# Two MoE blocks on one core: the chosen experts' rows are added to the shared expert's part by accumulating transfers instead of by GpSimd

## The chip, the cores and the metric

The kernel runs on one core of one Trainium2 chip. The time is the device time of one execution in microseconds; the median over a few executions is given, and one further execution was recorded by the hardware profiler. Engine names are those of the profile: PE is the matrix engine, PEld its weight loads, DVE the vector engine, ACT the scalar engine, POOL is GpSimd, SP the queue that issues most transfers. An entry such as SPq or POOLq is the queue of that engine.

## What is computed

The input is 32 sequences of 256 tokens with 128 features, so 8192 tokens. Two layers follow one another. Each normalises x, forms an attention part s and a mixture-of-experts part g, and adds their product to x. Cut to what matters here:

```
xn = layernorm(x)
s  = linear_attention(xn)              # layer 0: 16 heads, causal product of two scores
shared   = 0.1 * (gelu(xn @ sw_up + sb_up) @ sw_down + sb_down)
combined = sum over the 2 chosen of 8 experts of 0.1 * weight * expert(xn)
out = shared + combined
g   = silu(out / (max|out| + 1e-6))
x   = x + s * g
xn = layernorm(x)
s  = sparse_softmax_attention(xn)      # layer 1
g  = silu(mixture_with_capacity(xn))   # layer 1, top 2 of 8 experts
x  = x + s * g
```

The change touches the line `out = shared + combined` of layer 0 and the order of the work around it.

## The kernel before, in words

The tokens are cut into NP = 16 blocks of PT = 512 tokens; a block is a tile of 128 partitions with TT = 4 rows of 128 features, 128x512 numbers or 256 KB. Layer 0 goes like this.

**Attention of layer 0** (`attention0`) is one generator that is advanced in 256 small steps, 16 for each block. A step holds some transposes and products on PE, copies on ACT (`qk`, line 777) and multiplications on DVE (`feat`, line 744; `pat`, line 792). The whole kernel is written as such generators, and the code advances them in turn. Attention writes s and the shared expert's part of each block to DRAM as `part[p]`.

**Routing and dispatch** send each token's row to both chosen experts by indirect transfers from the POOL queue.

**The experts** (`experts`) take 71 tiles of 256 rows, and scatter the weighted results with indirect transfers (line 166) to `moe0` in DRAM, which has one row for each token and choice: first choice in rows 0 to 8191, second choice after them. Every reader of `moe0` has to wait for all these scatters (`back0.behind`).

**The combination of layer 0** (`combine0(p)`, one generator for each block) is where the change lies. It runs beside the last 40 steps of attention0, and for its last blocks beside the first steps of layer 1's attention. Its stages before the change are:

- stage 0: SP loads `x` (line 571), `so` with s and the shared part (line 965, 512 KB), and by `read` both rows of `moe0` into the tile `rows` (line 244, two transfers of 256 KB);
- stage 1: POOL adds the two to the shared part, `acc`, in the upper half of `so` (line 971, two instructions);
- stage 2: DVE forms the maximum and its reciprocal, `mx` (lines 974 to 977);
- stage 3: ACT scales `acc` (line 981) and takes the tanh (line 983) into the first half of `rows`; POOL multiplies s by `acc` (line 984);
- stage 4: DVE forms s times g (line 986), POOL adds x (line 987) and stores the new x to `x1` in DRAM (line 988);
- stages 5 to 7: the layernorm of layer 1: statistics on DVE (993 to 997), a power on POOL (998), the shift on DVE (`lnnb`, 1001), the scaling on ACT (1004);
- stages 8 and 9: transposes on PE (1009), and the routing logits of layer 1 (1019, 1021).

When each stage is written into the instruction streams is given by a plan: stage n of block p comes EVERY*p + LATER[n] steps after the experts' end.

```
EVERY, LATER = 3, (0, 3, 5, 6, 9, 10, 11, 13, 14, 16)
plan = sorted((t0 + EVERY * p + d, p, n) for p in range(NP) for n, d in enumerate(LATER))
```

PE, ACT and DVE keep this order: `inline` ties each instruction to the one written before it on its engine, so an instruction that waits holds up all behind it, those of attention0 too. POOL's instructions and SP's transfers are not tied in this way. A scheduler places them when the kernel is built, by when it believes their data to be there. On the chip each queue then runs strictly in that order.

The tiles `so` and `rows` come from a pool with four buffers. The `so` of block p+4 can be loaded only when line 987 of block p is done with the old one, and `rows` when line 986 is.

After the last block's logits, `route1` does the routing of layer 1; its dispatch and its experts follow, beside attention.

Of the kernel before, what the change touches and what calls it, by code (L numbers as in the profile page):

```python
# [11 lines left out]
F32 = mybir.dt.float32  # L12
# [3 lines left out]
ALU = mybir.AluOpType  # L16
# [4 lines left out]
P = 128  # L21
# [7 lines left out]
PT = 512  # L29
TT = PT // P  # L30
# [27 lines left out]
def model_kernel(ctx: ExitStack, tc: tile.TileContext, a: dict, out: bass.AP):  # L58
    nc = tc.nc
    B = a["x"].shape[0]  # L60
    T = B * S
# [18 lines left out]
    moe0 = dram.tile([2 * T, P], F32, name="moe0")  # L80
# [3 lines left out]
    moe = dram.tile([2 * T, P], F32, name="moe")  # L84
# [155 lines left out]
    def read(back, rows, moe, p):  # L240

        for k in range(2):
            t0 = k * T + p * PT
            get = nc.sync.dma_start(rows[:, k], moe[t0 : t0 + PT, :].rearrange("(n p) c -> p n c", p=P))
            back.behind(get)


    recent = {}
# [7 lines left out]
    def inline(made):  # L256


        if made.ins.engine in recent:
            tc.add_manual_dep(made.ins, recent[made.ins.engine].name, ORDER, reason="in the order given")  # L260
        return note(made)
# [22 lines left out]
    def mm_tile(name):  # L284
        return ps_m.tile([P, 512], F32, tag="mm", name=name)
# [256 lines left out]
    with ExitStack() as c0:  # L542
# [26 lines left out]
        def load(p):  # L569
            x = wk.tile([P, TT, P], F32, tag="x", name="x", bufs=6)  # L570
            nc.sync.dma_start(x, xin[:, p * TT : (p + 1) * TT, :])
            return x
# [123 lines left out]
        back0 = Scatter("results0", moe0)  # L696
# [263 lines left out]
        def combine0(p):  # L960

            t = slice(p * TT, (p + 1) * TT)
            x = load(p)
            so = bk.tile([P, 2, TT, P], F32, tag="soin", name="soin")
            nc.sync.dma_start(so, part[p])
            rows = bk.tile([P, 2, TT, P], F32, tag="rows", name="rows")
            read(back0, rows, moe0, p)
            yield
            acc = so[:, 1]
            for k in range(2):  # L970
                nc.gpsimd.tensor_tensor(acc, acc, rows[:, k], ALU.add)
            yield
            mx = wk.tile([P, TT], F32, tag="mx", name="mx", bufs=4)
            inline(nc.vector.tensor_reduce(mx, acc, AX.X, ALU.max, apply_absolute_value=True))
            inline(nc.vector.tensor_scalar(mx, mx, 1e-6, None, ALU.add))
            inline(nc.vector.reciprocal(mx, mx))
            inline(nc.vector.tensor_scalar(mx, mx, 0.5, None, ALU.mult))
            yield

            for i in range(TT):  # L980
                inline(nc.scalar.activation(acc[:, i, :], acc[:, i, :], AF.Copy, scale=mx[:, i : i + 1]))
            th = rows[:, 0]
            inline(nc.scalar.activation(th, acc, AF.Tanh))
            nc.gpsimd.tensor_tensor(so[:, 0], so[:, 0], acc, ALU.mult)
            yield
            inline(nc.vector.scalar_tensor_tensor(acc, th, 1.0, so[:, 0], ALU.add, ALU.mult))
            nc.gpsimd.tensor_tensor(x, x, acc, ALU.add)
            nc.gpsimd.dma_start(x1[p], x)
            yield
            st = wk.tile([P, TT, 6], F32, tag="lnst1", name="lnst1")  # L990
            mv = wk.tile([P, TT, 2], F32, tag="lnmv1", name="lnmv1", bufs=4)
            for i in range(TT):
                inline(nc.vector.bn_stats(st[:, i, :], x[:, i, :]))
            for i in range(TT):
                inline(nc.vector.bn_aggr(mv[:, i, :], st[:, i, :]))
            rs = wk.tile([P, TT], F32, tag="lnrs1", name="lnrs1", bufs=4)
            inline(nc.vector.tensor_scalar(rs, mv[:, :, 1], EPS, None, ALU.add))
            nc.gpsimd.tensor_tensor(rs, rs, minus[:, :TT], ALU.pow)
            yield
            nb = wk.tile([P, TT], F32, tag="lnnb1", name="lnnb1", bufs=4)  # L1000
            inline(nc.vector.scalar_tensor_tensor(nb, mv[:, :, 0], -1.0, rs, ALU.mult, ALU.mult))
            yield
            for i in range(TT):
                inline(nc.scalar.activation(xn[:, p * TT + i, :], x[:, i, :], AF.Identity,
                                            bias=nb[:, i : i + 1], scale=rs[:, i : i + 1]))
            yield
            pst1 = mm_tile("pst1")
            for i in range(TT):
                inline(nc.tensor.transpose(pst1[:, i * P : (i + 1) * P], xn[:, p * TT + i, :], ident))
            if p < KEEP:  # L1010
                xnT1 = xTs1[:, 2 * p : 2 * p + 2, EDGE : EDGE + S]
            else:
                xnT1 = wk.tile([P, PT], F32, tag="xnT1", name="xnT1").rearrange("p (b s) -> p b s", b=2)
            inline(nc.scalar.copy(xnT1, pst1.rearrange("p (b s) -> p b s", b=2)))
            yield
            psl = mm_tile("psl")
            pl = psl[:, : TT * E].rearrange("p (i e) -> p i e", e=E)
            for i in range(TT):
                inline(nc.tensor.matmul(pl[:, i, :], lhsT=xnT1[:, i // 2, i % 2 * P : (i % 2 + 1) * P], rhs=wg1,
                                        start=True, stop=True))  # L1020
            inline(nc.vector.tensor_copy(logit[:, t, :], pl))
            yield
# [66 lines left out]
        bk = c0.enter_context(tc.tile_pool(name="bk0", bufs=4))  # L1089


        EVERY, LATER = 3, (0, 3, 5, 6, 9, 10, 11, 13, 14, 16)
        t0 = at
        plan = sorted((t0 + EVERY * p + d, p, n) for p in range(NP) for n, d in enumerate(LATER))
        going = {}
# [3 lines left out]
        def results(now):  # L1099
            while plan and plan[0][0] < now and plan[0][1] <= (now - 4) // SPP - 1:  # L1100
                _, p, n = plan.pop(0)
                if n == 0:
                    going[p] = combine0(p)
                next(going[p])
# [64 lines left out]
    with ExitStack() as cm:  # L1169
# [38 lines left out]
        rows = [(e, e * CAP + q * MT) for e in range(E) for q in range(CAP // MT)]  # L1208
# [13 lines left out]
    with ExitStack() as cb:  # L1222
        bk = cb.enter_context(tc.tile_pool(name="bk", bufs=3))

        def combine(p):

            rows = bk.tile([P, 2, TT, P], F32, tag="rows", name="rows")
            read(back1, rows, moe, p)
            x = bk.tile([P, TT, P], F32, tag="xc", name="xc")
            nc.sync.dma_start(x, x1[p])  # L1230
            yield
            y = bk.tile([P, TT, P], F32, tag="yc", name="yc")
            helper = nc.gpsimd if p < NP - 1 else nc.vector
            helper.tensor_tensor(y, rows[:, 0], rows[:, 1], ALU.add)
            th = rows[:, 0]
            nc.scalar.activation(th, y, AF.Tanh)
            nc.scalar.activation(th, th, AF.Identity, bias=1.0)
            yield
            s = att.dst[p]
            helper.tensor_tensor(y, th, y, ALU.mult)  # L1240
            helper.tensor_tensor(y, y, s, ALU.mult)
            helper.tensor_tensor(y, y, x, ALU.add)
            nc.sync.dma_start(outv[:, p * TT : (p + 1) * TT, :], y)
            yield
# [115 lines left out]
```

## The time and the profile before

| | us |
|---|---|
| median of 3 runs | 1929.27 |
| lowest and highest | 1926.44 and 1931.02 |
| the profiled execution, its own time | 1932.48 |
| its span in the profile | 1930.6 |
| busy PE in that span | 1805.7 (94%) |
| busy DVE | 1175.4 (61%) |
| busy ACT | 962.0 (50%) |
| busy POOL | 847.5 (44%) |

The span is the time from the first to the last recorded instruction; 1.9 us of the execution's own time lie outside it. The combination of layer 0 stands between 940 and 1189 us of the span. A share of busy time is a mean over stages with different limits, so this stage has to be read by itself.

### The profile page before, as it was taken

The page shows a single profiled execution, that of the slowest core. Times are in us where ns is not written, and L with a number is a line of the kernel's source. Part 1 is how long each engine was busy: PE and PEld are TensorE (multiplying, and loading weights), DVE is VectorE, ACT ScalarE, POOL GpSimd, SP SyncE. Part 2 cuts the span into 40 slices and gives each one's busy share as a digit, 9 for nine tenths or more (in the row PEclk, how much of TensorE's full clock was granted, in tenths as well). Part 3 has the DMA queues.
Part 4 walks back from the last instruction along what each step waited for, and adds up shares of the span by engine and source line. Part 5 has one row for each costly group of instructions (what it writes and reads, how often), then busy time and mean ns, then how long its engine had stood idle before and what let it go on. Part 6 is the DMA issues. An engine that isn't in the chain of part 4 may idle for free.

```text
span 1930.6 us, 45909 instructions
## 1 busy us (share of the span) xinstructions
PE 1805.7 (94%) x18616; PEld 1394.5 (72%) x18616; DVE 1175.4 (61%) x2227; ACT 962.0 (50%) x2180; POOL 847.5 (44%) x991
## 2 busy tenths in 40 slices
PE   5999999998999999999887799999999799999997
PEld 4777777776888888887765676677777577777765
DVE  6659667665333433443577597888888433335786
ACT  5433333334444544545354575577677333335776
POOL 3001555543444544444545540044544355555454
PEclk8999999999999999999988777999999899999998
DMA  8911211112344443434334410211111122222343
GB/s 279 385 52 31 69 56 43 45 44 67 126 137 125 138 142 125 134 125 137 116 105 143 137 50 7 71 67 34 32 34 33 51 73 67 72 69 84 90 113 101
DMA packets 127524, 183.86 MB, mean 95 GB/s; under 512 B 16340, under 2 KB 83183, under 8 KB 127312
## 3 DMA queue, kind: packets, MB, share of 16 engines
q1 hardware_dynamic: 96096, 92.45, 16.2%
q0 software_dynamic: 28336, 79.73, 12.3%
q10 hardware_dynamic: 2880, 8.74, 1.2%
q8 instruction: 147, 2.41, 0.5%
q14 instruction: 65, 0.53, 0.1%
HBM read 104.11 MB, written 78.00 MB: 94 GB/s over the span
## 4 chain that ended last, share of the span: by engine, by line
PE 31%; ACT 8%; DVE 5%; DMA 2%; issue 2%; POOL 2%; SPq 1%; ACTq 0%; DVEq 0%; POOLq 0%
PE mpsu L1186 6%; PE mpsd L1200 6%; PE apsc L378 3%; PE apsT L406 3%; PE apav L415 3%; ACT apT L408 3%; ACT apr L398 2%; PE apsk L338 2%; PE apsc L384 2%; DMA rows<-moe 1%; PE apsq L350 1%; PE apsv L358 1%; PE mpst L1179 1%; DVE apr L396 1%; DMA soin<-part 1%
## 5 line engine op out<-in xcount | busy, mean ns | idle before, releaser
L166 POOL DMA_INDIRECT moe<-od,to x270 | 270.0, 1000 | 124.3 <-issue 70.8
L777 ACT COPY qk<-ptr 128x512 f32<-128x512 f32 x256 | 138.2, 588 | 241.9 <-PE ptr L775 241.4
L792 DVE TENSOR_TENSOR pat<-pp,dmask 128x1024 f32<-128x1024 f32 x128 | 156.2, 1221 | 109.6 <-PE pp L790 109.6
L395 DVE TENSOR_REDUCE amx<-apsc 128x4 f32<-128x496 f32 x256 | 170.2, 665 | 38.6 <-PE apsc L384 38.5
L408 ACT COPY apT<-apsT 124x512 f32<-124x512 f32 x256 | 142.8, 584 | 100.8 <-PE apsT L406 99.9
L790 PE MATMUL pp<-qk 64*128 64x128 f32 x2048 | 172.6, 297 | 15.8 <-DVE pat L792 14.1
L790 PEld LDWEIGHTS pp<-qk 64*128 64x128 f32 x2048 | 136.8, 194 | 58.4 <-issue 42.5
L396 DVE TENSOR_TENSOR apr<-apsc,amx 128x496 f32<-128x496 f32 x256 | 172.4, 673 | 9.1
L940 ACT ACTIVATE ha<-eup,wt 128x256 f32<-128x256 f32 x284 | 119.0, 471 | 111.8 <-PE eup L935 57.7
L935 PE MATMUL eup<-xdT,wt 128*128 128x256 f32 x568 | 150.2, 390 | 10.8 <-ACT od L954 7.1
L166 POOL DMA_INDIRECT disp<-xr,slot x128 | 132.4, 1034 | 62.7 <-issue 26.7
L744 DVE TENSOR_TENSOR feat<-rot 128x1024 f32<-128x1024 f32 x128 | 157.5, 1272 | 3.9
L406 PE MATMUL apsT<-ident,apr 128*124 128x128 f32 x1024 | 150.7, 293 | 8.3 <-ACT apr L398 3.5
L775 PE MATMUL ptr<-ident,feat 128*128 128x128 f32 x1024 | 146.9, 288 | 7.6 <-DVE feat L744 7.6
L166 POOL DMA_INDIRECT disp<-xr,sidx x128 | 126.7, 990 | 55.0 <-issue 24.7
L415 PE MATMUL apav<-ava,apT 124*64 124x9 f32 x4096 | 143.4, 205 | 0.0
L415 PEld LDWEIGHTS apav<-ava,apT 124*64 124x64 f32 x4096 | 136.8, 140 | 8.8 <-issue 8.4
L948 PEld LDWEIGHTS edn<-wt,ha 128*128 128x128 f32 x1136 | 137.8, 192 | 3.6
L948 PE MATMUL edn<-wt,ha 128*128 128x128 f32 x1136 | 138.1, 275 | 0.0
L775 PEld LDWEIGHTS ptr<-ident,feat 128*128 128x128 f32 x1024 | 114.7, 145 | 29.9 <-issue 13.9
L406 PEld LDWEIGHTS apsT<-ident,apr 128*124 128x124 f32 x1024 | 120.9, 148 | 16.2 <-ACT apr L398 8.8
L935 PEld LDWEIGHTS eup<-xdT,wt 128*128 128x128 f32 x568 | 99.5, 190 | 45.0 <-issue 27.4
(250 smaller groups left out, 3342.8 us busy)
## 6 DMA issues: line engine op xcount, KB each, us to landing
disp<-zero SPq DMA_DIRECT2D x17, 1040.0 KB, 8.5
rows<-moe SPq DMA_DIRECT2D x64, 256.0 KB, 3.9
xd<-disp SPq DMA_DIRECT2D x71, 130.0 KB, 2.3
xd<-disp SPq DMA_DIRECT2D x32, 260.0 KB, 2.8
x<-in_x SPq DMA_DIRECT2D x32, 256.0 KB, 4.6
moe<-zero SPq DMA_DIRECT2D x8, 1024.0 KB, 14.4
part<-so ACTq DMA_DIRECT2D x16, 512.0 KB, 3.5
soin<-part SPq DMA_DIRECT2D x16, 512.0 KB, 4.7
```

The costliest lines, as they stand in the source:

```text
L166: ins = order(lambda: nc.gpsimd.indirect_dma_start(out=self.dst[:, :], out_offset=bass.IndirectOffsetOnAxis(ap=idx, axis=0), in_=rows, in_ ...
L395: inline(nc.vector.tensor_reduce(mx, sv, AX.X, ALU.max))
L396: inline(nc.vector.tensor_tensor(to, sv, bc(mx, 2, NK), ALU.subtract))
L406: nc.tensor.transpose(psT[:NK, j, :], pr[:, 4 * g + j, :], ident)
L408: inline(nc.scalar.copy(pT[:NK], psT[:NK]))
L415: nc.tensor.matmul(avv[u * QB : (u + 1) * QB, h, :], lhsT=pT[:NK, j, u * QB : (u + 1) * QB], rhs=va[:NK, 2 * st + u, h, :], start=True, st ...
L744: inline(eng.tensor_tensor(f[:, n].rearrange("p (h i j) -> p h i j", i=D, j=D), bc(r[:, n], 3, D), bc(r[:, 2 + n], 2, D), ALU.mult))
L775: inline(nc.tensor.transpose(pst[:, 2 * n + c], seq.feat[c][:, n, m * P : (m + 1) * P], ident))
L790: inline(nc.tensor.matmul(pp[:, w, i, c], lhsT=qk[r, 2 + c], rhs=qk[r, c], start=True, stop=True))
L792: inline(nc.vector.tensor_tensor(pat.rearrange("p w i c q -> p (w i c) q"), pp.rearrange("p w i c q -> p (w i c) q"), bc(dmask, 1, 8), ALU ...
L935: nc.tensor.matmul(pu, lhsT=wt[:, f * P : (f + 1) * P], rhs=xdT, start=True, stop=True)
L948: nc.tensor.matmul(psd[:, s, :], lhsT=hl[:, f, s * P : (s + 1) * P], rhs=wl[:, FF + f * P : FF + (f + 1) * P], start=(f == 0), stop=(f == ...
```

## The change

The tile `rows` and its two loads by SP go away. In their place POOL issues two transfers for each block that read the rows from `moe0` and add them to `acc` in SBUF on the way (`accum_op`). The two write the same bytes, so the second waits for the first. Each has a stage of its own, so there are eleven stages, and the plan's offsets are new. `so` gets five buffers in place of four, and the tanh a small tile `th` of its own with two.

```
+    def fold(back, acc, moe, p, k):
+        t0 = k * T + p * PT
+        get = nc.gpsimd.dma_start(acc, moe[t0 : t0 + PT, :].rearrange("(n p) c -> p n c", p=P), accum_op=ALU.add)
+        back.behind(get)
...
-            so = bk.tile([P, 2, TT, P], F32, tag="soin", name="soin")
+            so = bk.tile([P, 2, TT, P], F32, tag="soin", name="soin", bufs=5)
             nc.sync.dma_start(so, part[p])
-            rows = bk.tile([P, 2, TT, P], F32, tag="rows", name="rows")
-            read(back0, rows, moe0, p)
             yield
             acc = so[:, 1]
             for k in range(2):
-                nc.gpsimd.tensor_tensor(acc, acc, rows[:, k], ALU.add)
-            yield
+                fold(back0, acc, moe0, p, k)
+                yield
...
-            th = rows[:, 0]
+            th = bk.tile([P, TT, P], F32, tag="th", name="th", bufs=2)
...
-        EVERY, LATER = 3, (0, 3, 5, 6, 9, 10, 11, 13, 14, 16)
+        EVERY, LATER = 3, (0,1,3,4,5,7,8,9,11,12,14)
```

## The prediction

> **What bounds the kernel now.** I read the page's shares first, then the clock's row and windows by stage, then the waits inside the stage that the change touches, then POOL's instructions there.
>
> ```profile
> PE 1805.7 (94%) x18616; PEld 1394.5 (72%) x18616; DVE 1175.4 (61%) x2227; ACT 962.0 (50%) x2180; POOL 847.5 (44%) x991
> PE   5999999998999999999887799999999799999997
> PEclk8999999999999999999988777999999899999998
> ...
> core 0: us, PE busy (x) PEld busy (x) DVE busy (x) ACT busy (x) POOL busy (x), PEclk, DMA share, GB/s
> 700.00:930.00 230.00, 224.80 (x1924) 188.37 (x1922) 85.52 (x140) 110.51 (x276) 111.22 (x135) 1.00 0.40 130
> 940.00:1100.00 160.00, 128.12 (x1281) 97.87 (x1280) 115.23 (x246) 74.65 (x184) 87.81 (x80) 0.87 0.47 138
> 1100.00:1210.00 110.00, 102.22 (x1045) 74.77 (x1043) 91.32 (x232) 74.18 (x156) 26.04 (x24) 0.74 0.10 32
> ```
>
> PE is the bound nearly everywhere: 98% busy at full clock from 700 to 930. The combination of layer 0 is the exception. From 940 to 1100 PE stands idle for 32 us of 160, and its clock is 0.87. So time can be won and lost here one for one. The 40 attention steps take about 152 us (940 to 1092), 3.8 us each, 11.5 us for each period of three steps, one block.
>
> ```profile
> POOL x L987 <- DVE soin L986: 24.1, 8, 8.2
> POOL soin L971 <- DMA soin<-part: 22.3, 11, 3.5
> PE pp L790 <- DVE pat L792: 13.4, 6, 4.5
> POOL soin L984 <- ACT soin L981: 13.4, 5, 5.4
> DVE lnnb L1001 <- POOL lnrs L998: 12.0, 5, 3.8
> DVE lnst L993 <- POOL x L987: 3.3, 3, 1.3
> ...
> 1056.39 1.26 POOL L971 TENSOR_TENSOR soin<-soin,rows 128x512 f32<-128x512 f32 x1 [3.45 <-DMA soin<-part]
> 1057.81 1.26 POOL L971 TENSOR_TENSOR soin<-soin,rows 128x512 f32<-128x512 f32 x1 [0.15 <-DMA rows<-moe]
> 1059.03 1.03 POOL L998 TENSOR_TENSOR lnrs<-lnrs,minus 128x4 f32<-128x4 f32 x1
> ...
> soin<-part SPq DMA_DIRECT2D x16, 512.0 KB, 4.7
> rows<-moe SPq DMA_DIRECT2D x32, 256.0 KB, 5.6
> x<-x POOLq DMA_DIRECT2D x12, 256.0 KB, 5.7
> ```
>
> The first lines are waits in that window (total, times, longest). DVE loses 12.0 + 3.3 = 15.3 us to a late POOL, and PE then waits for `pat` and `feat`, since DVE's order is fixed. The timeline lines show how POOL gets late: the sum waits 3.45 us for `soin` while the power (998), for which DVE waits, stands behind it. Nobody waits for the sums' result itself: they run some steps ahead of `mx`. What POOL holds up is what stands behind them. The last lines give the transfers' times to landing in this window.
>
> **The change part by part.** *Removed:* 32 sums. In the window 29 of them took 1.42 us each (their median over all is 1.27), 41 of POOL's 88 busy us. As nobody waits for their result, their end alone is worth little. They also stretch DVE: `feat` took 1.62 us on average in this window, 16 of them, against 1.22 between 500 and 700 us, +6.3 us; `rot` 0.63 against 0.42, +3.4; smaller ones (975, 977, 997, 1001, 986) some 7 more. Of these 17 us the sums' share of POOL's arithmetic (41 of 82) is 8 us. DVE was 72% busy, so I count half: **-4 us**. SP's 32 loads of `rows` go too; SP issues were 0.4 us each, and SP waited mostly for buffers. Nothing.
>
> *Buffers and plan:* `so` with five buffers is loaded one block further ahead; the tanh's own tile takes away the wait for `rows`. The waits that remain before the first fold of a block are like those before the sums, 22 us. The new plan writes `mx` one step after the second fold and 986 two steps after `mx`'s scaling, where there were three. The last logits come about two steps earlier, but `route1` begins at the same attention step, and PE's order there has the same work. Nothing; if that cover failed, one step, 4 us.
>
> *Added:* 32 transfers on POOL. The order of the built program shows what stands between the first and second fold of a block. First come ten folds of five blocks, alternating. Then blocks 5 to 15 have one pair each in POOL's order. For blocks 6, 8, 9, 10 and 15 nothing stands between; elsewhere 998 and 984 (2.3 us: 5, 11), 984 (1.3: 7, 13), or 987 and 988 (2.2: 12, 14). That is 11.6 us in all. The second fold waits for the first to land, and POOL with it.
>
> No accumulating transfer is in this trace. Issue: the 128-piece store on POOL took 0.62 us, an indirect transfer 0.98; a fold has 512 pieces of 512 B; I take 1.0. Landing: from 3.9 (the loads of the same rows over the whole run, outside this crowd) to 7.8 (twice that, as the destination is read too). I take **5.6**, that of the same rows in this window; the POOL store of 256 KB beside it took 5.7. An accumulate that is faster than a plain load has no reason.
>
> A rule is to be weighed here: the Trainium skill, "DMA: Bandwidth & Descriptors", section "Anatomy of one DMA — SWDGE (gpsimd) path", gives a transfer issued by GpSimd about 2.0 us plus its bytes at 436 GB/s. For 256 KB that is 2.6 us by the page's figures, an estimate. The rows in this stage show over twice that, and they decide. With 2.6, a fold would keep POOL only 1.6 us beyond its issue, the six pairs with work between them would cost next to nothing, and the change would be worth the -4 us above.
>
> One speaks against the change: "SBUF — State Buffer", section "Who interferes with whom", says that a transfer seen stalled by DVE was one whose descriptors GpSimd writes, since DVE's two-port modes lock it out. Up to one DVE instruction (1.2 us) for each of 32 issues would be +38 us at the very worst. The 16 stores on POOL, all in or just after this stage, took between 0.60 and 0.67 us with DVE 72% busy. The row says nothing is lost, so I add nothing.
>
> *POOL's budget* for the eleven periods from the first 987 (973.1 us) to the twelfth (1112.7), 139.6 us. Own work for each block: 1.28 + 1.27 + 0.30 + 0.62 + 1.03 = 4.5, so 49.5. Before: sums 11 x 2.54 = 28, waits for loads 22; 99.5 in all, and 40 us in which POOL waited for DVE and ACT (24.1 + 13.4 of it in the lines above). After: issues 22; waits for first folds 11 x (5.6 - 1.0) - 11.6 = 39; waits for loads 21; 131.5 in all. So POOL would still fit into 139.6, but with 8 us of slack for 40.
>
> *Which of these waits hit a deadline.* I walked POOL's order block by block against DVE's plan: 993 one step after 986, 1001 two steps after it. At 3.85 us a step and 5.5 a landing, with the delays carried on: 987 of block 1 and 998 of block 0, 1.0 together; 987 of block 2 behind the pair of block 6, 3.1; 987 of 3 and 4 behind those of 7 and 8, 0.95 and 0.9; 998 of block 4 behind the pair of block 9, 8.3; 987 and 998 of block 6 behind the pairs of 10 and 11, 3.3 and 2.85; 998 of block 8 behind the second fold of 12 and the pair of 13, 6.5; 987 of block 11 behind the pair of 15, 3.1. The largest, for example: 987 of block 4 ends at 0; `soin` of block 9 lands 4.7 later; its folds start at 4.7 and 10.2; 998 ends at 12.2, and DVE wanted it at 3.9. Sum 30 us, in the place of 15.3 now: **+15**.
>
> The ten folds at the start: from 947.5 (first sum before) with alternating waits, the last is issued about 20 us later, at 967; 984 of block 0 then ends at 968.3, and DVE's 986 is due at 967 to 970. **+1 to +2**. [...] in five of the 20 batches here 16 `pp` products took 2.08 us instead of 1.16, about 1 us for each; two or three more, **+2**.
>
> Sum: -4 + 15 + 1 + 2 = +14 us on the profiled execution's 1932.5, so 1946.5. That execution was 3.2 above the median; from the median 1929.3 the change gives **1943**.
>
> **The rivals.** *Faster, because a fold lands soon.* If a fold lands in about 3.9 us, POOL's waits for first folds fall from 39 to about 20, the walk's stalls to about 12 us, and -4 + 12 - 15.3 makes -7; a clock that recovers can double it, 1915. It decides below about 4.3 us of landing. For it: the stage has 32 us of idle PE to give, and SP no longer sends three large loads at once, so the crowd thins. Against: the second source, and the store on POOL at 5.7.
>
> *Much slower: POOL becomes the bound.* At 7.8 us of landing, or with an issue of 2 us, the budget is 131.5 + 24 = 155, over the 139.6 there are, before any deadline; with these +30 to +40, 1965. For it: 512 pieces where the trace has 128 on this queue.
>
> *No change: the slack takes it.* 131.5 is still under 139.6; if DVE's own delays shift with POOL's, the stalls replace those of now, 1929. Against: the places named above have deadlines of one or two steps, and 998 of block 4 and of block 8 have a whole pair before them.
>
> *The change does not do what it says:* if sums or loads of `rows` were still there under another name. The built order has neither left, so this has no share.
>
> **How the numbers follow.** A measurement here can tell about 0.2% from no change, 3.9 us. The walk's case (+5 to +25) has 0.45, the bound POOL (+25 to +45) 0.17, no change 0.10, faster 0.28. So slower 0.62, same 0.10, faster 0.28. The forecast is the walk's, 1943. For the range I leave out the fastest and the slowest tenth: 1916 (-13) to 1964 (+35). Signs are mixed, so beside it the likeliest case's own range: 1934 to 1954.
>
> **What would show it.** Right: folds that land 5 to 6.5 us after issue; POOL waits of 4 to 5 us before second folds, near 39 us in all; DVE's `lnnb` waiting for 998 and `lnst` for 987 for about 30 us together, longest near 8 at the fifth block; the end of attention0 10 to 20 us later, and all after it shifted; `feat` near 1.4 us. Wrong: landings under 4.3 us, or DVE waits for POOL under 15 us; then the stage shortens, with PE's idle time under 32 us. Folds over 8 us, or DVE's `mx` waiting for a fold itself, mean the bound POOL.

## The result, and the profile after

The changed kernel takes **1942.19 us** (median of 9; lowest 1933.21, highest 1951.99). Beside it the kernel before took 1927.79 (9 runs). The ratio is 1.0075, 95% interval 1.005 to 1.01: slower by 14.4 us. The profiled execution took 1937.85 us, 5.4 more than that of before and 4.3 under its own median, so positions inside the trace carry some microseconds of chance.

The page of after first: shares, PE's busy row and granted clock, and the fold's transfer line (KB each, us from issue to landing).

```profile
PE 1798.7 (93%) x18616; PEld 1391.0 (72%) x18616; DVE 1178.1 (61%) x2227; ACT 961.3 (50%) x2180; POOL 848.1 (44%) x991
PE   5999999998999999999877788999999999999987
PEclk8999999999999999999987789899999999999998
...
soin<-moe POOLq DMA_DIRECT2D x32, 256.0 KB, 4.8
```

The shares are those of before, and POOL's busy time too (848.1 against 847.5): the 32 folds keep POOL as long as the 32 sums did. A share of busy time shows nothing of this change. The clock's low slices come earlier, but are no more than in before's row. The windows by stage of after:

```profile
core 0: us, PE busy (x) PEld busy (x) DVE busy (x) ACT busy (x) POOL busy (x), PEclk, DMA share, GB/s
700.00:930.00 230.00, 224.98 (x1923) 188.40 (x1922) 85.73 (x140) 110.90 (x277) 111.22 (x134) 1.00 0.40 130
940.00:1100.00 160.00, 119.56 (x1167) 94.00 (x1167) 105.71 (x225) 67.08 (x168) 77.47 (x68) 0.83 0.65 127
```

Up to the combination nothing has moved. In the combination PE is busy 119.6 of 160 us (128.1 before), does 1167 products (1281 before), and its clock is 0.83 (0.87). The waits of after between 940 and 1120 us (total, times, longest):

```profile
POOL soin L250 <- DMA soin<-moe: 38.3, 14, 4.7
POOL soin L250 <- DMA soin<-part: 30.6, 10, 5.8
DVE lnnb L1005 <- POOL lnrs L1002: 26.5, 7, 8.2
PE pp L796 <- DVE pat L798: 21.4, 6, 7.4
DVE soin L990 <- POOL soin L988: 12.8, 2, 9.2
DVE lnst L997 <- POOL x L991: 4.1, 2, 2.1
```

Line 250 is the fold; 988, 990, 991, 997, 1002 and 1005 of after are 984, 986, 987, 993, 998 and 1001 of before. The first line is new: POOL stands 38.3 us in second folds that wait for first ones. DVE now waits 26.5 + 12.8 + 4.1 = 43.4 us for a late POOL, where it waited 15.3, and PE waits behind DVE (21.4 for `pat`, 13.4 before). One such place, from the timeline of after (start, duration, engine and line, in brackets the idle time and its releaser):

```profile
1034.22 1.31 POOL L250 DMA_DIRECT2D soin<-moe  x1 [3.75 <-DMA soin<-part]
1039.35 1.27 POOL L250 DMA_DIRECT2D soin<-moe  x1 [3.81 <-DMA soin<-moe]
1040.12 1.57 POOL L1002 TENSOR_TENSOR lnrs<-lnrs,minus 128x4 f32<-128x4 f32 x1
...
1041.73 0.16 DVE L1005 SCALAR_TENSOR_TENSOR lnnb<-lnmv,lnrs 128x4 f32<-128x4 f32 x1 [8.20 <-POOL lnrs L1002]
```

The power of block 4 on four numbers per partition stands behind both folds of block 9. They cost POOL two waits and two issues, and DVE stands 8.2 us. In the lines of before shown with the prediction, a power (at 1059.03 us) stood behind one wait of 3.45 us and two sums.

How far attention falls behind can be read from PE's batches of 16 `pp` products, 20 in the 40 steps. Two of them in the timeline of before:

```profile
963.40 2.08 PE L790 MATMUL pp<-qk 64*128 64x128 f32 x16 [1.59 <-DVE pat L792]
971.43 1.16 PE L790 MATMUL pp<-qk 64*128 64x128 f32 x16
```

The same two in the timeline of after:

```profile
962.12 2.08 PE L796 MATMUL pp<-qk 64*128 64x128 f32 x16 [5.96 <-ACT qk L783]
976.45 2.08 PE L796 MATMUL pp<-qk 64*128 64x128 f32 x16
```

After is 1.3 us ahead at the first and 5.0 behind at the second: the ten folds at the start lie between them. The 8.2 us wait shown above takes the lag from 7.3 to 14.3 us (batches at 1025.34 and 1043.17, in before 1018.03 and 1028.89), and at the last batch it is 17.4 (1103.40 against 1085.98).

The end of attention0 shows in the first product of `route1` (line 222): 1226.5 us after, 1213.2 before, 13.3 later. From 940 to there PE stood idle 61.3 us instead of 39.9, and was busy 225.2 us instead of 233.3 for about as many products, at a granted clock of 0.85 against 0.82. So 21.4 us were lost in waiting, and 8.1 came back because PE ran faster. By the first `mpst` product of layer 1's experts the profiled execution is only 4.6 later (1523.5 against 1518.9). The change touches nothing between these two points. That stretch took 305.7 us in before, 297.0 in after and 295.8 to 305.8 in the other traces, so before's is at the long end; why is open. The medians differ by 14.4.

### The profile page after: what moved, and what is told of

Same layout as the page of the kernel before. It is cut to its first block, busy times and chain, and to the rows that moved or that the text cites. A ratio compares the mean times of both kernels' runs of the same rounds, so it can differ in the third digit from the quotient of the medians.

```text
span 1936.0 us, 45871 instructions
## 1 busy us (share of the span) xinstructions
PE 1798.7 (93%) x18616; PEld 1391.0 (72%) x18616; DVE 1178.1 (61%) x2227; ACT 961.3 (50%) x2180; POOL 848.1 (44%) x991
## 4 chain that ended last, share of the span: by engine, by line
PE 33%; ACT 7%; DMA 6%; DVE 6%; issue 3%; POOL 3%; ACTq 0%; DVEq 0%; POOLq 0%; SPq 0%
PE mpsu L1190 6%; PE mpsd L1204 6%; PE apsT L412 3%; PE apav L421 3%; PE apsc L384 3%; ACT apT L414 3%; DMA soin<-part 3%; DMA soin<-moe 3%; ACT apr L404 2%; PE eup L941 2%; PE apsk L344 1%; PE apsc L390 1%; DVE apr L402 1%; DVE amx L401 1%; PE edn L954 1%
## 5 line engine op out<-in xcount | busy, mean ns | idle before, releaser
L796 PEld LDWEIGHTS pp<-qk 64*128 64x128 f32 x2048 | 138.5, 196 | 72.0 <-issue 30.6
L166 POOL DMA_INDIRECT disp<-xr,sidx x128 | 128.1, 1000 | 53.5 <-POOL breath L150 26.9
```

Source lines behind the costliest of these rows:

```text
L166: ins = order(lambda: nc.gpsimd.indirect_dma_start(out=self.dst[:, :], out_offset=bass.IndirectOffsetOnAxis(ap=idx, axis=0), in_=rows, in_ ...
L796: inline(nc.tensor.matmul(pp[:, w, i, c], lhsT=qk[r, 2 + c], rhs=qk[r, c], start=True, stop=True))
```

## The experiments

Kernels were timed beside runs of the kernel before on their own chip (its medians: 1927.8, 1930.5, 1932.5 and 1924.2 us), so ratios are compared; "us" is the ratio's distance from 1 times 1927.8. The last column is the first product of line 222, which marks the end of the stage (1213.2 in before). It comes from one profiled execution, and the order of two kernels in it can differ from that of their medians: e3's marker is 4.2 us later than before's, its median 5 lower.

| kernel | median | ratio to before (95%) | us | end of stage |
|---|---|---|---|---|
| after | 1942.2 | 1.0075 (1.005 to 1.01) | +14 | 1226.5 |
| e1_split: accumulates, no wait | 1914.9 | 0.9912 (0.988 to 0.9944) | -17 | 1203.7 |
| e2_plain: overwrites, with wait | 1911.5 | 0.9899 (0.9876 to 0.9922) | -19 | 1192.9 |
| e9_split_plain: overwrites, no wait | 1896.2 | 0.9858 (0.983 to 0.9886) | -27 | 1184.7 |
| e4_neither: no folds, no sums | 1899.4 | 0.9835 (0.9808 to 0.9862) | -32 | 1184.9 |
| e8_before_nosum: before, no sums | 1901.2 | 0.9836 (0.9806 to 0.9865) | -32 | 1184.1 |
| e5_wideplan: after, offsets near the old | 1948.8 | 1.0088 (1.0061 to 1.0115) | +17 | 1233.8 |
| e3_pinned: after, POOL in written order | 1925.2 | 0.9976 (0.9959 to 0.9992) | -5 | 1217.4 |
| e6_pinned2: the same, folds earlier | 1907.4 | 0.9864 (0.9834 to 0.9895) | **-26** | 1191.3 |
| e7_before_pinned: before, POOL in written order | 1920.8 | 0.994 (0.9907 to 0.9974) | -12 | 1207.2 |
| e10_before_pinned2: the same, sums at the step of e3's second fold | 1917.6 | 0.9965 (0.9941 to 0.9989) | -7 | 1210.8 |

**The wait alone (e1_split).** The second fold adds into the other half of the tile, so it has nothing to wait for.

```
-                fold(back0, acc, moe0, p, k)
+                fold(back0, so[:, 1 - k], moe0, p, k)
```

> The changed kernel, but the second fold of a block adds into the other half of the tile, where s lies, so that it need not wait for the first to land (the sum is then left out in that form: the second row goes into s). Same two transfers, same plan. Theory A (POOL's queue is held by the wait of the second fold for the first): POOL's waits for folds, 42 us in the changed kernel, fall to about nothing, DVE's waits for POOL (27 + 13 + 4 us) to 15 or less, and the time from 1942 to 1930 or less. Rival B (the transfers themselves cost it: 1.3 us of issue each and twice the reading): 1938 to 1942. Rival C (the new plan with its shorter distances costs it): 1936 to 1942.

It fell to 0.9912, 31 us under after. The waits of e1_split, same stretch:

```profile
POOL soin L250 <- DMA soin<-part: 24.5, 8, 7.4
DVE lnnb L1005 <- POOL lnrs L1002: 19.9, 8, 6.3
DVE soin L990 <- POOL soin L988: 3.4, 1, 3.4
```

POOL's waits for folds are gone, and DVE waits 23.3 us for POOL in place of 43.4, though not the 15 or less that was expected. The edit also let the scheduler bring four of the eleven later pairs together (blocks 5, 11, 12 and 13: what stood between the two folds in after follows the second here); what that is worth by itself was not measured. Accumulation's price in issue remains. Ten folds stand back to back at the start. The timeline of e1_split, where the second number is their joint duration:

```profile
951.97 13.15 POOL L250 DMA_DIRECT2D soin<-moe  x10 [6.26 <-PE ptr L781]
```

The same place in the timeline of e9_split_plain (told below), where the folds overwrite:

```profile
948.44 7.56 POOL L250 DMA_DIRECT2D soin<-moe  x10 [6.30 <-PE ptr L781]
```

1.31 us each with accumulation, 0.76 without.

**The accumulation alone (e2_plain).** Both folds overwrite; POOL's order in the trace is that of after, and the wait stays.

```
-        get = nc.gpsimd.dma_start(acc, moe[...], accum_op=ALU.add)
+        get = nc.gpsimd.dma_start(acc, moe[...])
```

> The changed kernel with both folds as plain transfers that overwrite the destination (the additions are left out, and with them the second read). Everything else stays, the second's wait for the first too. Theory A: landing is bounded from below by a plain load, 4 to 4.8 us, so the waits stay near 35 us and the time at 1936 to 1942. Rival B, if the accumulation is what costs: landing falls to 3 us or less and the time to 1930 or less.

0.9899, 34 us under after: what theory A said of it was wrong, and the time is rival B's, though a landing of 3.4 us is not its "3 us or less". The folds' own row in e2_plain (duration in ns least/median/most, then us to landing):

```profile
L250 POOL DMA_DIRECT2D soin<-moe x32: 747/752/832, 946.4 to 1094.4; - x32
DMA to landing us min/median/max: 3.0/3.4/5.1
```

The waits of e2_plain, same stretch as above:

```profile
POOL soin L250 <- DMA soin<-moe: 29.1, 14, 3.9
DVE lnnb L1005 <- POOL lnrs L1002: 15.6, 9, 3.1
DVE soin L990 <- POOL soin L988: 3.4, 1, 3.4
```

The same row of after has 1274/1310/2919 and 4.5/4.8/8.0. So accumulating costs 0.56 us more of POOL and 1.4 us more to land, for the same bytes. POOL still waits 29.1 us for first folds here, but DVE's longest wait for it is 3.4 us, not 9.2: what counts is how late POOL is at a deadline, not the sum of its waits.

**Both (e9_split_plain), and no folds at all (e4_neither).** e9 has both edits; e4 leaves out the call of `fold`.

> This kernel has both edits of e1_split and e2_plain: the second fold goes to the other half of the tile (so it waits for nothing) and both folds overwrite instead of accumulating, so the routed rows are not added. It closes a table of two by two: accumulate with wait 1942, accumulate without wait 1915, overwrite with wait 1911, overwrite without wait is this one. Theory A, the wait and the accumulation cost independently of each other: the wait is worth 27 us and the accumulation 31, so this would be 1942 - 58 = 1884, below even the kernel with no folds at all (1899), which it cannot be; so A would show as close to 1900. Theory B, both act through one thing, the lateness of GpSimd, which has room again once either is taken away: 1905 to 1912, little below the better of the two. In the trace: no GpSimd waits for a fold, the fold's issue at 0.75 us and its landing at 3.4 to 4 us, and VectorE's waits for the row statistics at lnnb at 9 to 15 us.

> The changed kernel without folds: the experts' rows are not read and not added, the stages of the plan stay. It shows what the stage has to give. Theory A: DVE's waits for POOL under 8 us, and 1915 to 1925, 3 to 12 below the kernel before, since POOL then has neither sums nor waits. Rival C: 1934 or more, as the plan is the same.

e4's 1899 is below the 1915 to 1925 expected: the stage had more to give than was thought. With the wait taken away, accumulation costs 27 - 17 = 10 us; with it, 34. With overwriting, the wait costs 27 - 19 = 8 us; with accumulation, 31. The two are not additive: 8 and 10 alone, 42 together. DVE's waits for POOL between 940 and 1120 us go the same way: 12.1 us in e9, 19.0 with the wait alone (e2), 23.3 with the accumulation alone (e1), 43.4 with both. POOL is late at some of DVE's deadlines with either one, and at far more with both. e9's own time, 1896, missed the 1905 to 1912 of its second theory and fell near the floor that the first one named; it is the table that speaks against independent costs. Between e9 and e4 lie 4 us, with overlapping intervals: 32 plain transfers that wait for nothing cost next to nothing.

**The sums in before (e8_before_nosum).** The two sums are left out of before; SP still loads the rows.

```
-            for k in range(2):
-                nc.gpsimd.tensor_tensor(acc, acc, rows[:, k], ALU.add)
```

> The kernel before without its sums (both rows are loaded, but not added). The run with neither sums nor folds was at 1899, 31 below the kernel before. If the sums on POOL are all of that, this is at 1897 to 1904, with DVE's multiplications at their undisturbed 1.22 us. If the loads and their crowd on SP's queue, or the shorter plan, have a part in it: 1908 to 1920.

It gave 0.9836, as e4 did. So the sums cost before 32 us (26 to 37). And since e4 has no loads of `rows`, five `so` buffers, the tile `th` and the new offsets, these four together are worth nothing measurable without sums or folds. Waits of e8_before_nosum (its lines 985, 991, 996 and 999 are 987, 993, 998 and 1001 of before):

```profile
DVE lnst L991 <- POOL x L985: 3.5, 4, 1.3
DVE lnnb L999 <- POOL lnrs L996: 3.2, 3, 1.5
```

DVE's waits for POOL fall from 15.3 to 6.7 us, and `feat` from 1616 ns to 1369 (4 us over 16), not to the 1.22 us expected. These two make 13 of the 32. PE's rows show where the time went: from 940 us to the marker, 29.1 us sooner in e8, PE was idle 27.4 us instead of 39.9, and busy 216.7 instead of 233.3 for about as many products, at a granted clock of 0.90 instead of 0.82. Of the batches of 16 `pp` products five took 2.08 us in before, one in e8. So over half of the gain in these two executions is PE running faster, not PE waiting less; what lowered the clock in before is not shown.

**The plan's offsets (e5_wideplan).** Changed kernel, later offsets; this was the theory that the closer plan is to blame.

```
-        EVERY, LATER = 3, (0,1,3,4,5,7,8,9,11,12,14)
+        EVERY, LATER = 3, (0,2,3,5,6,9,10,11,13,14,16)
```

> The changed kernel with the plan spread to the distances of the kernel before, (0,2,3,5,6,9,10,11,13,14,16): one step more between the loads and the first fold, one between the second fold and the maximum, one between the product and the last sum. POOL's order stays the scheduler's. Theory A (second folds hold POOL's queue): the pairs stay adjacent, waits for folds stay near 40 us, 1934 to 1946. Rival C (the shorter plan costs it): 1930 or less.

1.0088: no better than after, and 3 us above the range written down for theory A. Its waits:

```profile
POOL soin L250 <- DMA soin<-moe: 36.1, 12, 4.7
DVE lnnb L1005 <- POOL lnrs L1002: 23.5, 6, 9.7
DVE lnst L997 <- POOL x L991: 18.1, 6, 7.5
```

POOL waits for folds about as long as in after, and DVE gets late POOL at other places: 41.6 us in all. The close plan falls as a cause. Offsets alone move the deadlines, but not POOL's own order.

**POOL's order (e3_pinned, e6_pinned2).** `fold` returns its transfer, and POOL's five kinds of instruction are tied to the written order with `inline`, as DVE's are. Then the offsets decide what stands before what. Nothing is left out of the computation.

```
+                inline(fold(back0, acc, moe0, p, k))
...
+            inline(nc.gpsimd.tensor_tensor(rs, rs, minus[:, :TT], ALU.pow))
...
-        EVERY, LATER = 3, (0,1,3,4,5,7,8,9,11,12,14)
+        EVERY, LATER = 3, (0,2,5,7,8,10,11,12,14,15,17)   # e3
+        EVERY, LATER = 3, (0,1,4,7,8,10,11,12,14,15,17)   # e6
```

Both put a block's two folds three steps apart, one period, so that the first can land before the second comes.

> The changed kernel with POOL's instructions of the combination tied to the plan's order, and the plan spread to (0,2,5,7,8,10,11,12,14,15,17), so that between the two folds of a block stands a whole period with the power, the product and the sum of other blocks. Theory A: POOL waits for folds under 10 us, DVE's waits for POOL under 15 us, 1920 to 1930; if so it is a kernel that keeps the change and loses nothing. Rival B: 1938 to 1942. Rival C: also faster, as the plan is longer; the next runs would have to tell A from C.

> The third run again (POOL tied to the plan's order), with the folds a step earlier, so that the maximum stands three steps behind the second fold in place of two: (0,1,4,7,8,10,11,12,14,15,17). There DVE waited 24 us for the folds' landing and ended at 1925. Theory A: that wait falls under 6 us, and the time to 1905 to 1918, below the kernel before. If POOL's issues (1.3 us each) or the transfers' traffic are a cost of their own: 1922 to 1928 still.

e3 moved the wait instead of removing it. POOL waits only 5.5 us for folds there, but in e3_pinned DVE has these waits:

```profile
DVE mx L978 <- DMA soin<-moe: 24.4, 9, 5.3
DVE lnnb L1005 <- POOL lnrs L1002: 6.4, 6, 1.2
```

One such place in the timeline of e3_pinned:

```profile
1013.87 1.04 POOL L1002 TENSOR_TENSOR lnrs<-lnrs,minus 128x4 f32<-128x4 f32 x1 [5.23 <-DVE lnrs L1001]
1016.10 2.62 POOL L250 DMA_DIRECT2D soin<-moe  x2
1020.62 0.69 DVE L978 TENSOR_REDUCE mx<-soin 128x4 f32<-128x512 f32 x1 [2.72 <-DMA soin<-moe]
```

In e3's order the power and the product stand before the folds, and POOL waits for the power's data first, 47.8 us in all. Here the folds start 1.8 us before DVE wants `mx` (at 1017.90), and they land after 5.9 us (median). e6 writes the second fold one step earlier. That puts both folds ahead of the power in POOL's order and three steps ahead of `mx`; POOL's waits for the power's data fall to 13.6 us. It takes 1907.4 us, 0.9864 of before: it beats both kernels. The waits of e6_pinned2:

```profile
POOL soin L250 <- DMA soin<-moe: 10.8, 4, 5.2
DVE lnnb L1005 <- POOL lnrs L1002: 13.6, 10, 1.8
DVE mx L978 <- DMA soin<-moe: 1.1, 2, 0.9
```

And two lines of its timeline:

```profile
1022.03 2.66 POOL L250 DMA_DIRECT2D soin<-moe  x2
1027.18 1.04 POOL L1002 TENSOR_TENSOR lnrs<-lnrs,minus 128x4 f32<-128x4 f32 x1 [2.49 <-DVE lnrs L1001]
```

Two folds of different blocks follow one another without a wait, and the power after them is ready before its data is: here POOL waits 2.49 us for DVE, not DVE for POOL. Accumulation itself is no cheaper than in after (1.42 us of issue, 6.7 us to land); little that is urgent stands behind it.

**Order alone (e7_before_pinned, e10_before_pinned2).** Before, its sums kept, with the same ties; e7 with the old offsets, e10 with (0, 5, 7, 8, 10, 11, 12, 14, 15, 17).

> The kernel before, with its sums, and POOL's instructions of the combination tied to the plan's order. If the sums too hold POOL because the scheduler put them ahead of the power while their loads were still on the way (22 us of waiting for the loaded tile), these waits and DVE's 15 us for POOL go: 1912 to 1924. If the sums' own time on POOL and its disturbance of DVE is what they cost: 1926 to 1932.

> The kernel before, with its two sums per block on GpSimd, but with GpSimd tied to the written order and with the power of the row statistics put ahead of the sums, as in e6_pinned2. It computes the reference. It tells whether e6_pinned2 (1907) is fast for its order or for its folds. If the order alone does it: 1905 to 1910. If the sums cost by themselves, by GpSimd's time and by what they do to VectorE beside them (feat near 1.7 us against 1.2 in e6): 1915 to 1922, near e7_before_pinned's 1921.

0.994 and 0.9965. These two orders are worth 12 and 7 us to before. Neither is e6's, although e10 was meant to be: with the sums at step 5, POOL runs power, product, sums, as in e3, where e6 runs folds, power, product. Like with like, e10 (0.9965) and e3 (0.9976) can't be told apart. Sums in e6's order (step 4) were not run, so how much of e6's 26 us belongs to the folds and how much to its order stays open.

What the sums do to DVE can be seen. In e10 and e6 its groups of `feat` differ (busy us, mean ns). From the groups of e10_before_pinned2, 940 to 1100 us:

```profile
L744 DVE TENSOR_TENSOR feat<-rot 128x1024 f32<-128x1024 f32 x16 | 24.9, 1596 | 0.6
```

And from those of e6_pinned2:

```profile
L750 DVE TENSOR_TENSOR feat<-rot 128x1024 f32<-128x1024 f32 x16 | 18.9, 1222 | 0.6
```

With the sums `feat` takes 374 ns more, 6 us over 16; in e6 it takes what it took outside the stage. That is not so in every order: in after, with the same folds, it took 1435 ns. In e10 `mx` also waits 7.0 us for the sums, but e6 waits 7.2 more at `lnnb` (13.6 against 6.4). So 6 of the 19 us between the two kernels are accounted for; the rest is open.

## Why the prediction came out right, point by point

**The forecast.** 1943 was predicted, slower; 1942.2 was measured. The mechanism, POOL waiting between a block's folds while DVE's small needs stand behind, is shown by e1 and e2: take the wait away, or make the folds cheaper, and 31 or 34 us go. That the number was met within 1 us is luck: several terms of the sum were off and cancelled.

**Removed: -4 for relief.** This step failed in size. e8 shows that the sums cost before 32 us; the sum credited it with 4, and with the 15.3 us of old stalls that it set against the new ones, 19 in all. The 4 us for the stretched DVE were too few: `feat` alone, one of the rows it counted, gave 4 in e8. Another error was to take the old stalls as the only wait that the sums cause, and to give them no part in PE's clock (0.82 to the marker, 0.90 without them). In after `feat` took 1435 ns against 1616, about the 1.4 us foretold: 2.9 us.

**Added: +15 net, 30 of DVE stalls.** The waits it named came out closely: `lnnb` 26.5 and `lnst` 4.1 make 30.6 us, the longest 8.2 at the fifth block (8.3 in the walk). Place by place, 24.3 us stand where the walk had 26.0; 6.3 stand at the powers of blocks 2, 5 and 10, which it had free; and its 4.0 at the sums of blocks 4 and 11 did not come. The 12.8 us at `soin` are in no term of the walk. Underneath, landing was overestimated (5.6; measured 4.8) and issue underestimated (1.0; measured 1.31), so that a wait after issue is 3.8 us, not 4.6. POOL's waits for first folds were put at 39 for eleven pairs. Over the whole trace they are 41.9, but 10.4 of them belong to the ten folds at the start; the pairs have 31.5. Waits for `soin` were 30.6, not 21; its 512 KB landed in 5.6 us instead of 4.7.

**The ten folds at the start: +1 to +2.** Too small. Their times were right: begun at 945.7, the last issued at 967.9. The due time was not: DVE stood for block 0's 990 from 961.3, not from 967 to 970. The timeline of after:

```profile
967.94 1.28 POOL L250 DMA_DIRECT2D soin<-moe  x1 [2.98 <-DMA soin<-moe]
968.71 1.80 POOL L988 TENSOR_TENSOR soin<-soin 128x512 f32<-128x512 f32 x1
...
970.54 0.69 DVE L990 SCALAR_TENSOR_TENSOR soin<-th,soin 128x512 f32<-128x512 f32 x1 [9.25 <-POOL soin L988]
```

The plan writes line 990 at step 7, where before had it at step 9: 7.6 us earlier at 3.8 a step. The walk used the old due time. Not all of the 9.25 us is lost: against before's start of that instruction (972.3) less the 7.6, 970.5 is 5.8 us late, an estimate, and the `pp` batches on either side lose 6.3 (from 1.3 ahead to 5.0 behind).

**The whole of the added side.** From e4 (no folds, the rest of the change in place) to after is 0.9835 to 1.0075, 46 us. The prediction's added terms were 30 + 1.5 + 2 = 33.5. So the removed side was 13 us too small and the added side about as much: the net of +14 was met because these cancelled.

**Slack.** Part of the new stalls replaced old ones, as the rival "no change" had it: in the two traces DVE's waits for PE at `so`, `tu` and `pat` fell from 11.6 + 6.6 + 3.4 to 8.0 + 2.8 + 0.3 us, 10.5, while those for POOL rose by 28. It was not enough.

**Buffers, SP's loads and the clock.** Buffers and loads were counted at nothing, and e4 beside e8 bears it out. The clock's +2 came out in its own terms: seven batches took about 2 us in after, five in before, where two or three more were foretold. A gap before a batch does not decide it: in before one of the five had no wait before it, and a batch after a wait of 2.87 us took 1.16. And the batches are not the clock's whole part: from 940 to 1100 it was 0.83 in after against 0.87, but from 1100 to 1210 it was 0.87 against 0.74, so that over the whole way to the marker the clock helped after. That attention0 would end 10 to 20 us later came true (13.3); that all behind it would be shifted by as much did not, in this execution (4.6 at `mpst`).

**The rules weighed.** The estimate of 2.6 us worked out from the Trainium skill, "DMA: Bandwidth & Descriptors", section "Anatomy of one DMA — SWDGE (gpsimd) path", was set aside for the row, 5.6. A plain fold took 3.4, an accumulating one 4.8: both lie between. The rival that rested on early landing put its point at 4.3 us. e2, at 3.4 but also with the cheaper issue, was indeed faster, by 19 us where the rival had 7 to 14. The other rule, descriptors locked out by DVE, was rightly given nothing: in after the 256 KB store took 0.62 us on average as in before (624 ns against 621), with DVE 66% busy from 940 to 1100.

**POOL as the bound.** It did not come true as a whole. (For an issue of 2 us its sum of 155 does not follow: the issues add 22, but the waits after them lose 11, so it is 142.5, still over the 139.6.) But e1, e2 and e9 show it in small: POOL had too little room between two deadlines, not over the stage.

## What to carry to other kernels

A transfer that accumulates in place of an engine's sum takes the arithmetic away but not the issue, and two of them onto the same bytes put a landing into the issuing queue. Give the first a whole period to land before the second is written, fix the queue's order by hand, and look at what small, urgent instruction stands behind the pair (e3 and e6 did these together, not one by one): the same 32 folds came out 14 us over the kernel before in one order, 5 under it in a second and 26 under it in a third. The kernel with the sums gains from an order too (7 to 12 us here), so compare each at its best order. Judge such a change by the waits of the engines that depend on the queue, not by its busy share, which did not move here (848.1 against 847.5 us).

## What the runs showed that was not expected

- Accumulation costs the issuing engine, not only the transfer: POOL's issue of 256 KB rose from 0.75 to 1.31 us and landing from 3.4 to 4.8 us (e2_plain against after). An accumulating issue takes as long on POOL as the sum that it replaces (median 1.27).
- An accumulating issue's record overlaps the next arithmetic's on POOL: at 1039.35 the fold is recorded with 1.27 us, yet the power starts 0.77 later and takes 1.57 in place of 1.04. The end is where the two durations one after the other would put it (1041.69 against 1041.66), so nothing is gained by it.
- Accumulating folds that follow one another without a wait land later: 6.0 us in e1_split and 6.7 in e6_pinned2 against 4.8 in after. Plain ones do not: 3.5 in e9_split_plain, 3.4 in e2_plain.
- The sums on POOL cost 32 us in before, though nobody waits for their result and POOL was busy for 88 of 160 us in that stage. Over half of it, in the traces, is PE busy for longer at a lower granted clock.
